# A two-stage fused kernel on one core: cross-partition sums and maxima moved off GpSimd, and a new table of durations in its list scheduler

## The chip, the core and the metric

The kernel runs on one core of a Trainium2 chip. The metric is the device time of one execution in microseconds (us), lower is better. Engines are named as the profile names them: PE is TensorE (matmul), DVE is VectorE, ACT is ScalarE, POOL is GpSimd, SP is SyncE, which here issues every DMA. Each engine works through its own instructions in order and waits on semaphores for the others.

## What is computed

Two residual steps over `x` of 2 batches x 1024 tokens x 2048 features:

```python
def fake_quant(x, scale, zp):
    q = jnp.clip(jnp.round(x / s + z), 0.0, 255.0)
    return (q - z) * s

# step 1: quantized product with the context
x = x + matmul(fake_quant(layernorm(x), x1_scale, x1_zp),      # (2, 1024, 2048)
               fake_quant(ctx_4096, x2_scale, x2_zp))          # (2, 2048, 2048)

# step 2: a dense layer with 8 low-rank experts, the best 2 per token
xf = layernorm(x)
probs = softmax(xf @ W_router.T)
topk_p, topk_i = top_k(probs, 2); topk_p = topk_p / sum(topk_p)
h = einsum('td,erd->ter', xf, lora_A)
lora_out = einsum('ter,eor,te->to', h, lora_B, w) * 2.0        # w: topk_p at topk_i
x = x + (xf @ W_base.T + b_base) + lora_out
```

`W_base` is 2048 x 2048, `lora_A` 8 x 16 x 2048, `lora_B` 8 x 2048 x 16, all f32.

## The kernel before

**Tiling.** A tile is 128 tokens; there are 8 per batch (`NT`), taken in 4 pairs (`NP`, index `p`). The output columns are cut in four of 512 (`C`), or two halves of 1024 (`HD`, index `cp`).

**First gemm.** For each token tile `load_x` and `ln1` load `x`, take the statistics on DVE (`bn_stats`), refine the reciprocal square root with three Newton steps (on DVE for the very first tile, on POOL for the others, L576 to L586), quantize to `q` (uint8, ACT only), subtract the zero point to `qn` (f16, ACT or DVE), and transpose with a DMA to `at`. For each column block `load_b` loads a pair of context rows `bs`, quantizes to `u` (uint8, L626, DVE only) and subtracts the zero point to `b` (f16, ACT or DVE, L627). `gemm1` multiplies (`g`, L636) and adds into `x` on DVE (L657), `square` on ACT gathers the sum of squares for the second layer norm.

**Between.** `ln2` makes the scale and shift of the second layer norm per pair (statistics on DVE, Newton on POOL except for the last pair). `y_prep` makes, per pair, six operand tiles for a Strassen-like second gemm: normalized quarters `yt`, sums and differences of them (`comb`, L749), and from each a high and a low f16 part in `nat` (L740 and L742), transposed by a DMA to `y` (L744). `x` goes to DRAM as `spill` where its buffers are needed. That makes 24 large transposes per batch.

**Second gemm.** For each half `cp` of the columns come four groups `grp` of products (`GROUPS`), each over 8 steps `k`. `w_step` loads rows of `W_base` (`wt`, `wb`, `ws`), combines them on DVE (L918, L928, L932, L939, L942) and splits them into a high and a low f16 part scaled by `gW` (`hi`, ACT or DVE; `lo`, DVE, L902). `g2` multiplies (L1032), adds the low-rank part (L1046), and evicts on DVE (L1057) into `xr` or `x`. `hmm` makes the router and low-rank products (L790, L794), `router` picks the experts.

**The scales.** `gW` is a power of two from the largest sum of squares of `W_base` rows and from the largest `lora_B`. `prep_bmax` takes the largest absolute value per partition on DVE (L484, L488), then the maximum over the 128 partitions with a custom POOL instruction (L491, `partition_all_reduce`), and `fin` makes `lB` from it (L497 to L502). `w_norm(cp)` squares every row of one half of `W_base` (`wn`, `wj`, L525 and L527), sums along the row on DVE (L534), sums over partitions with the same custom POOL instruction (L537), and makes `gW`, `uW`, `sB` (L542 to L549). Every `hi` and `lo` of that half, and every eviction L1057, needs them. It runs once before the second gemm of batch 0 and once, for the other half, in group 3 of its first half.

**The order.** Nothing is issued in program order. `Plan.add` collects tasks with engine, duration and buffers, and `Plan.order` is a list scheduler in the program: `rank` gives each task a latest start from the due times of PE's tasks, and the loop keeps a clock, a busy time per engine, and a count of free buffers per tag (48 of tag `u`, 8 PSUM banks). At every event each free engine takes the most urgent ready task whose buffers are free. A task with two possible engines (`affine` without `only`) goes to ACT if ACT is idle at that instant, else to DVE. The instructions are then issued in order of planned start, so a planned start fixes each engine's queue; semaphores keep the real execution right where it runs later than planned. For a DMA the plan keeps `dma_free`, the time at which the DMA engines have moved all that was issued; SP issues no further one while that is more than 2.5 us (`DEPTH`) ahead or 8 (`LANES`) are in flight.

The old times for a DMA, at L242 and in the two helpers:

```python
dma_free = max(now + 1.1, dma_free) + t.dma
t.done = dma_free + 2.0
# load:      SP 0.47, dma = bytes / 360e3
# transpose: SP 1.25, dma = 0.896 * cols / 1024
```

Of the kernel before, what the change touches and what calls it, by code (L numbers as in the profile page):

```python
# [11 lines left out]
F32 = mybir.dt.float32  # L12
# [54 lines left out]
DMA_SLACK = 3.0  # L67

# [14 lines left out]
class Task:  # L83
    __slots__ = ("eng", "dur", "durs", "fn", "preds", "succs", "prio", "cap", "bufs", "left",
                 "ready", "start", "done", "dma", "seq", "pe", "far", "need")


class Plan:
# [3 lines left out]
    def add(self, eng, dur, fn, r=(), w=(), prio=None, cap=None, dma=None, far=None):  # L92
# [7 lines left out]
        t.far = far  # L100
# [40 lines left out]
    def order(self):  # L141
# [6 lines left out]
        dma_free = 0.0  # L148
        lag = 0.0
# [43 lines left out]
        while todo:  # L193
# [8 lines left out]
            for eng in busy:  # L202
                while busy[eng] <= now:
# [35 lines left out]
                    end = now + t.dur  # L239
                    busy[eng] = end  # L240
                    wake(end)
                    if t.dma is not None:  # L242
                        dma_free = max(now + 1.1, dma_free) + t.dma
                        t.done = dma_free + 2.0
                        lanes = [x for x in lanes if x > now] + [t.done]
                    else:
                        t.done = end + 0.2
# [22 lines left out]
def xattn_ffn_kernel(ctx, tc, x, cx, scal, wT, bias, arT, bT, out):  # L270
# [41 lines left out]
    nc.gpsimd.memset(magic, 0x5F3759DF)  # L312
    iota = const.tile([P, E], F32)
# [17 lines left out]
    def load(dst, dst_ap, src, nbytes, w, r=(), **kw):  # L331
        add("SP", 0.47, lambda: nc.sync.dma_start(dst_ap(), src() if callable(src) else src),
            r=r, w=w, dma=nbytes * P / 360e3, **kw)

    def transpose(dst, src, r, w, cols, **kw):
        add("SP", 1.25, lambda: nc.sync.dma_start_transpose(dst(), src()),
            r=r, w=w, dma=0.896 * cols / 1024, **kw)

    def affine(dst, src, n, r, w, scale=None, bias=None, only=None, **kw):
# [19 lines left out]
        durs = {"ACT": n * 0.00083 + 0.19 + 0.09 * ptrs, "DVE": n * 0.00053 + 0.08 + 0.06 * ptrs}  # L359
# [49 lines left out]
    def prep_lora(when):  # L409
        a32 = []  # L410
        ps = bank("arn")
        on = buf("u", [P, P], F32, "ones")
        add("POOL", 0.2, lambda: nc.gpsimd.memset(on.ap(), 1.0), w=[on])
        for q in range(4):
# [11 lines left out]
            def mm(q=q, s=v):  # L426
                for k in range(4):
                    nc.tensor.matmul(
                        ps.ap()[:, :AR], on.ap(), s.ap()[:, k, :], start=q + k == 0,
                        stop=q + k == 6,  # L430
                    )

            add("PE", 1.0, mm, r=[v, on], w=[ps], prio=when + q)
# [35 lines left out]
        for q in range(2):  # L469
# [3 lines left out]
            add("DVE", 0.6,  # L473
# [4 lines left out]
    def prep_bmax():  # L478
        m = buf("sm", [P, 52], F32, "sm_bmax")
        for h in range(2):  # L480
            s = buf("u", [P, HD], F32, f"bms_{h}")
            load(s, s.ap, bT[:, h * HD : (h + 1) * HD], HD * 4, [s])
            add("DVE", 1.13,
# [6 lines left out]
        add("POOL", 1.5,  # L490
            lambda: nc.gpsimd.partition_all_reduce(  # L491
                b_max, m.ap()[:, 2:3], P, bass_isa.ReduceOp.max), r=[m], w=[bmax_b])

        def fin():
            a = m.ap()
            i = a[:, 3:4].bitcast(I32)
# [7 lines left out]
        add("DVE", 0.8, fin, r=[lora_b], w=[m, bmax_b])  # L504
# [8 lines left out]
    def w_norm(cp, when):  # L513
        acc = buf("wacc", [P, 24], F32, f"wacc_{cp}", KT)
        for n, k in enumerate(range(KT - 1, -1, -1)):
# [6 lines left out]
            def sq(eng, s=s, d=d, k=k):  # L522
# [8 lines left out]
            add({"ACT": 1.2, "DVE": 1.3}, 0, sq, r=[s], w=[d, (acc, [k])],  # L531
# [4 lines left out]
        add("POOL", 1.5,  # L536
            lambda: nc.gpsimd.partition_all_reduce(  # L537
                acc.ap()[:, 21:22], acc.ap()[:, 20:21], P, bass_isa.ReduceOp.add), w=[acc])

        def fin():  # L540
            a = acc.ap()
            pow2(a[:, 22:23], a[:, 21:22], a)  # L542
# [8 lines left out]
        add("DVE", 1.5, fin, r=[bmax_b, lora_b], w=[acc, (scale_b, [cp])])  # L551
# [14 lines left out]
    def ln1(S, b, i):  # L566
# [3 lines left out]
        for h in range(2):  # L570
            add("DVE", 1.2, lambda h=h: stats(xt[h], s, 0, h), r=[xt[h]], w=[s])
# [43 lines left out]
    def load_b(S, b, c):  # L615
        for j in range(4):
            bp = buf("u", [P, 4, C], F16, f"b_{b}_{c}_{j}", 2)
            S["b", c, j] = bp
            for h in range(2):
# [6 lines left out]
                affine(u.ap, s.ap, HD, [s], [u], scale=r2, bias=z2, only="DVE")  # L626
# [3 lines left out]
    def gemm1(S, b, i, c, t):  # L630
# [30 lines left out]
        add("DVE", 0.78, evac, r=[ps], w=[(xb, [c % 2]), (s, [j])], cap=t + KT * MM + EV1)  # L661
# [21 lines left out]
        add("ACT", 1.3, lambda: square(c // 2), r=[xb], w=[(s, [j]), sq])  # L683
# [41 lines left out]
    def y_prep(S, b, p):  # L725
# [10 lines left out]
        def emit(o, t):  # L736
# [4 lines left out]
            add("DVE", 1.13,  # L741
# [6 lines left out]
        def comb(dst, a, c, op):  # L748
            add("DVE", 1.13, lambda: nc.vector.tensor_tensor(dst.ap(), a.ap(), c.ap(), op),  # L749
# [438 lines left out]
```

## Time and profile before

| | us |
|---|---|
| median of three runs | 966.87 |
| lowest, highest run | 965.12, 968.43 |
| span of the profiled execution | 965.8 |

What the page adds, of the lines not shown further on:

| part of the page | what it says |
|---|---|
| granted PE clock in tenths, by the 40 slices | 7 in the second slice (24 to 48 us), 9 in all others |
| chain that ended last, share by engine | PE 62%, DVE 19%, POOL 6%, DMA 5%, issue 5%, ACT 2%, SP queue 1% |
| DMA queue | 225,456 packets, 242.33 MB, 83.0% of 16 engines' span |
| u, L357 on DVE | 64 instructions, 808 ns each |
| b, L346 on ACT | 47 instructions, 1143 ns each |
| q, L346 on ACT | 32 instructions, 1232 ns each |
| nat by L742, 1024 wide, on DVE | 56 instructions, about 1217 ns each |
| landing of a 512 KB load, from issue | 6.4 (wt) to 9.9 (bs) us |
| landing of a transpose, from issue | 4.3 to 5.9 us |

A row of a timeline gives start, duration, engine, line, operation, what it writes and reads, and, in brackets, the idle time of the engine before it with what ended that. SPq is SP's queue: its duration is the time for which the DMA instructions held the queue. Several like instructions in a row are merged (x5). In a table of windows each engine's busy time stands beside the count of its instructions.

### The profile page before, as it was taken

Reading aid. Unit: us, or ns where it says so; the run is one execution under the profiler, and the core shown is the slowest. Engines: PE = TensorE matmul, PEld = TensorE weight load, DVE = VectorE, ACT = ScalarE, POOL = GpSimd, SP = SyncE. Lnnn points to the kernel's source line nnn. Section 1 sums busy time; section 2 is a strip of 40 time slices with the busy share of each in tenths; the row PEclk is TensorE's granted clock in tenths of the full one; section 3 lists DMA queues with packets and bytes.
Section 4 is the critical chain, followed back from the end, with each engine's and each line's share of the span. In section 5 each row is a group of like instructions: output and inputs, shape, how many; then the busy total and the mean of one; then the engine's idle time right before and its main releaser. Section 6 shows DMA issues by size and latency. Waiting matters only on the chain.

```text
span 965.8 us, 12426 instructions
## 1 busy us (share of the span) xinstructions
PE 913.9 (95%) x4478; PEld 431.5 (45%) x4478; DVE 734.1 (76%) x1229; ACT 379.9 (39%) x440; POOL 100.0 (10%) x353
## 2 busy tenths in 40 slices
PE   3699998997999999999999999997898999999998
PEld 1245445454444444444444444545543444444443
DVE  7579887996988876999555778987597876699231
ACT  3466785641425422243555644641230321225000
POOL 3405431000000000005220223000000000000000
PEclk9799999999999999999999999999999999999999
DMA  9999999899899986966999979899978479695011
GB/s 319 246 392 336 303 313 243 214 189 233 246 302 389 360 312 244 363 219 242 239 273 356 319 190 228 245 215 185 255 180 262 163 272 325 207 356 171 34 66 66
DMA packets 225518, 243.12 MB, mean 252 GB/s; under 512 B 160944, under 2 KB 162992, under 8 KB 225456
## 3 DMA queue, kind: packets, MB, share of 16 engines
q1 hardware_dynamic: 225456, 242.33, 83.0%
q8 instruction: 35, 0.57, 0.2%
q14 instruction: 27, 0.22, 0.1%
HBM read 172.03 MB, written 31.46 MB: 211 GB/s over the span
## 4 chain that ended last, share of the span: by engine, by line
PE 62%; DVE 19%; POOL 6%; DMA 5%; issue 5%; ACT 2%; SPq 1%; DVEq 0%; POOLq 0%; ACTq 0%
PE X L1032 28%; PE Y L1032 19%; PE g L636 11%; DVE yt_a L749 2%; DVE nat_s L742 2%; DVE w L902 2%; PE X L1046 2%; PE Y L1046 2%; DVE nat_a L742 2%; DMA wb<-in_wT_dram 2%; DVE xr L1057 1%; POOL sm L399 1%; POOL sm L395 1%; DMA wt<-in_wT_dram 1%; DVE x L657 1%
## 5 line engine op out<-in xcount | busy, mean ns | idle before, releaser
L636 PE MATMUL g<-b,at 128*128 128x512 f16 x1024 | 228.5, 386 | 9.2 <-ACT b L346 7.4
L1032 PEld LDWEIGHTS <-y_s 128*128 128x128 f16 x1536 | 149.8, 98 | 192.4 <-issue 9.9
L1032 PE MATMUL Y<-w,y_s 128*128 128x512 f16 x768 | 207.1, 380 | 5.7 <-DVE hf L809 2.8
L1032 PE MATMUL X<-w,y_s 128*128 128x512 f16 x768 | 207.7, 381 | 4.3 <-DVE w L902 2.6
L1032 PE MATMUL X<-w,y_a 128*128 128x512 f16 x768 | 190.4, 380 | 4.5 <-DVE w L902 2.6
L1032 PEld LDWEIGHTS <-y_a 128*128 128x128 f16 x1152 | 112.5, 98 | 144.9 <-issue 7.3
L636 PEld LDWEIGHTS <-at 128*128 128x128 f16 x1024 | 101.4, 99 | 133.6 <-issue 17.5
L346 ACT ACTIVATE w<-wb,gW 128x1024 f16<-128x1024 f32 x59 | 67.4, 1147 | 190.3 <-DVE wb L932 94.3
L1032 PE MATMUL Y<-w,y_a 128*128 128x512 f16 x384 | 103.3, 379 | 3.8 <-DVE xr L1057 2.7
L902 DVE SCALAR_TENSOR_TENSOR w<-wb,gW,w 128x1024 f16<-128x1024 f32 x64 | 81.6, 1278 | 11.7 <-ACT w L346 11.3
L357 DVE TENSOR_SCALAR u<-bs,rec,sc 128x1024 uint8<-128x1024 f32 x64 | 50.9, 808 | 27.5 <-DMA bs<-in_cx_dram 22.0
L346 ACT ACTIVATE b<-u,nz 128x1024 f16<-128x1024 uint8 x47 | 53.0, 1143 | 44.7 <-DVE u L357 40.2
L1057 DVE SCALAR_TENSOR_TENSOR xr<-X,uW,xr 128x512 f32<-128x512 f32 x70 | 50.5, 744 | 25.7 <-PE X L1046 23.2
L1057 DVE SCALAR_TENSOR_TENSOR xr<-Y,uW,xr 128x512 f32<-128x512 f32 x45 | 33.2, 742 | 36.0 <-PE Y L1046 36.0
L657 DVE SCALAR_TENSOR_TENSOR x<-g,s,x 128x512 f32<-128x512 f32 x64 | 47.4, 745 | 10.3 <-PE g L636 10.1
L346 ACT ACTIVATE q<-x,sm 128x1024 uint8<-128x1024 f32 x32 | 38.0, 1232 | 34.0 <-POOL sm L584 29.2
L928 DVE TENSOR_TENSOR wb<-wt 128x512 f32<-128x512 f32 x32 | 21.9, 687 | 34.4 <-DMA wt<-in_wT_dram 28.7
L939 DVE TENSOR_TENSOR wb<-wb,wt 128x1024 f32<-128x1024 f32 x32 | 38.7, 1218 | 11.5 <-DMA wb<-in_wT_dram 11.5
L742 DVE TENSOR_TENSOR nat_s<-yt_a,nat_s 128x1024 f16<-128x1024 f32 x32 | 38.3, 1217 | 5.5 <-ACT nat_s L346 5.5
L367 DVE BATCH_NORM_STATS2 sm<-x 128x6 f32<-128x512 f32 x64 | 40.4, 680 | 2.5 <-DMA x<-in_x_dram 2.4
L346 ACT ACTIVATE nat_s<-yt_a 128x1024 f16<-128x1024 f32 x27 | 27.8, 1049 | 33.3 <-DMA y_s<-nat_s 14.9
L790 PE MATMUL ph<-ar,y_a 128*128 128x272 f16 x192 | 37.0, 284 | 3.9 <-DVE xr L1057 2.1
(157 smaller groups left out, 901.8 us busy)
## 6 DMA issues: line engine op xcount, KB each, us to landing
wt<-in_wT_dram SPq DMA_DIRECT2D x88, 512.0 KB, 6.4
bs<-in_cx_dram SPq DMA_DIRECT2D x64, 512.0 KB, 9.9
wn<-in_wT_dram SPq DMA_DIRECT2D x32, 512.0 KB, 7.6
wb<-in_wT_dram SPq DMA_DIRECT2D x32, 512.0 KB, 8.1
x<-in_x_dram SPq DMA_DIRECT2D x30, 512.0 KB, 8.3
spill<-x SPq DMA_DIRECT2D x28, 512.0 KB, 4.0
xr<-spill SPq DMA_DIRECT2D x28, 512.0 KB, 6.8
out_dram<-xr SPq DMA_DIRECT2D x24, 512.0 KB, 4.2
```

The lines of the kernel that those rows point to most:

```text
L346: nc.scalar.activation(o, i, AF.Copy if c is None else AF.Identity, scale=1.0 if a is None else a, bias=0.0 if c is None else c,)
L357: nc.vector.tensor_scalar(o, i, a, c, ALU.mult, ALU.add)
L367: nc.vector.bn_stats(st[:, 2 * h + c], b.ap()[:, c * C : (c + 1) * C])
L636: nc.tensor.matmul(ps.ap(), aT.ap()[:, k, :], S["b", c, k // 4].ap()[:, k % 4, :], start=k == 0, stop=k == KT - 1,)
L657: nc.vector.scalar_tensor_tensor(xs, ps.ap(), s12, xs, ALU.mult, ALU.add, accum_out=s.ap()[:, o : o + 1])
L742: lambda: nc.vector.tensor_tensor(n.ap()[:, 1], t.ap(), n.ap()[:, 0], ALU.subtract), r=[t], w=[n])
L790: nc.tensor.matmul(ph.ap()[:, : 2 * AR], y[half].ap()[:, 0, k, :], ar[:, kr, :], start=kk == 0, stop=False,)
L902: lambda: nc.vector.scalar_tensor_tensor(w.ap()[:, 1, lo:up], src(), g, w.ap()[:, 0, lo:up], ALU.mult, ALU.subtract),
L939: lambda: nc.vector.tensor_tensor(bot.ap(), bot.ap(), top.ap(), ALU.subtract),
L1032: nc.tensor.matmul(ps.ap(), y.ap()[:, a, k, :], w.ap()[:, q, j * C : (j + 1) * C], start=k == 0 and fresh and i == 0, stop=k == HK - 1 and ...
L1046: nc.tensor.matmul(ps.ap(), hT.ap()[:, 2 * p + tt, a], lb.ap()[:, q], start=False, stop=i == 2, skip_group_check=True,)
L1057: nc.vector.scalar_tensor_tensor(xs, ps.ap(), uW[:, cp : cp + 1], xs, ALU.mult, ALU.add)
```

## The change

Four things change together.

1. `w_norm`: the sum over partitions is a matmul of a constant 128x128 tile of ones (f32) with the column of partial sums, into a PSUM bank; `fin` reads the bank. The constant is set once at the start; `prep_lora` uses it instead of a tile of its own.
2. `prep_bmax`: the column of maxima is stored to DRAM, loaded back as one row broadcast to all partitions, and reduced by DVE along the row.
3. `load_b`: `u` may go to ACT or DVE.
4. The scheduler's times: a rate of 405e3 bytes per us for loads, landing times, a rule for transposes (flag `turn`: it holds SP until everything issued before has landed), and new durations for most tasks.

```diff
+RATE = 405e3
+LAND = 1.9
+TURN_LAND = 2.5
+NEXT = {"DVE": 0.08, "ACT": 0.1}
...
                     end = now + t.dur
+                    if t.dma is not None:
+                        if t.turn:
+                            end = max(end, land)
+                            dma_free = max(dma_free, end + t.dma)
+                            t.done = end + TURN_LAND
+                        else:
+                            dma_free = max(end + 0.2, dma_free) + t.dma
+                            t.done = dma_free + LAND
+                        land = max(land, t.done)
+                        lanes = [x for x in lanes if x > now] + [t.done]
+                    else:
+                        t.done = end + 0.1
+                        end -= NEXT.get(eng, 0.0)
                     busy[eng] = end
                     wake(end)
-                    if t.dma is not None:
-                        dma_free = max(now + 1.1, dma_free) + t.dma
-                        t.done = dma_free + 2.0
-                        lanes = [x for x in lanes if x > now] + [t.done]
-                    else:
-                        t.done = end + 0.2
...
+    ones = const.tile([P, P], F32)
+    nc.gpsimd.memset(ones, 1.0)
...
     def load(dst, dst_ap, src, nbytes, w, r=(), **kw):
-        add("SP", 0.47, lambda: nc.sync.dma_start(dst_ap(), src() if callable(src) else src),
-            r=r, w=w, dma=nbytes * P / 360e3, **kw)
+        add("SP", 0.42, lambda: nc.sync.dma_start(dst_ap(), src() if callable(src) else src),
+            r=r, w=w, dma=nbytes * P / RATE, **kw)
 
     def transpose(dst, src, r, w, cols, **kw):
-        add("SP", 1.25, lambda: nc.sync.dma_start_transpose(dst(), src()),
-            r=r, w=w, dma=0.896 * cols / 1024, **kw)
+        add("SP", 1.35 + 0.25 * cols / 1024, lambda: nc.sync.dma_start_transpose(dst(), src()),
+            r=r, w=w, dma=0.5 * cols / 1024, turn=True, **kw)
...
-        durs = {"ACT": n * 0.00083 + 0.19 + 0.09 * ptrs, "DVE": n * 0.00053 + 0.08 + 0.06 * ptrs}
+        durs = {"ACT": n * 0.00083 + 0.19 + 0.09 * ptrs, "DVE": n * 0.00053 + 0.145 + 0.06 * ptrs}
...
-        add("POOL", 1.5,
-            lambda: nc.gpsimd.partition_all_reduce(
-                b_max, m.ap()[:, 2:3], P, bass_isa.ReduceOp.max), r=[m], w=[bmax_b])
+        d = Buf("dram", lambda: dram.tile([P, 1], F32, name="bmax"))
+        row = buf("u", [P, P], F32, "bmax_row")
+        load(d, d.ap, lambda: m.ap()[:, 2:3], 4, [d], r=[m])
+        load(row, row.ap, lambda: d.ap().rearrange("p o -> o p").to_broadcast([P, P]), P * 4,
+             [row], r=[d])
 
         def fin():
             a = m.ap()
+            nc.vector.tensor_reduce(b_max, row.ap(), AX.X, ALU.max)
...
-        add("POOL", 1.5,
-            lambda: nc.gpsimd.partition_all_reduce(
-                acc.ap()[:, 21:22], acc.ap()[:, 20:21], P, bass_isa.ReduceOp.add), w=[acc])
+        ps = bank(f"wsum_{cp}")
+        add("PE", 0.2,
+            lambda: nc.tensor.matmul(
+                ps.ap()[:, :1], ones, acc.ap()[:, 20:21], start=True, stop=True),
+            r=[acc], w=[ps], prio=when + WN_STEP * KT)
...
-                affine(u.ap, s.ap, HD, [s], [u], scale=r2, bias=z2, only="DVE")
+                affine(u.ap, s.ap, HD, [s], [u], scale=r2, bias=z2)
...
-        add("DVE", 0.78, evac, r=[ps], w=[(xb, [c % 2]), (s, [j])], cap=t + KT * MM + EV1)
+        add("DVE", 0.75, evac, r=[ps], w=[(xb, [c % 2]), (s, [j])], cap=t + KT * MM + EV1)
...
-            add("DVE", 1.13,
+            add("DVE", 1.22,
                 lambda: nc.vector.tensor_tensor(
                     n.ap()[:, 1], t.ap(), n.ap()[:, 0], ALU.subtract), r=[t], w=[n])
```

The other durations move in the same manner: 1024-wide `tensor_tensor` and reduces on DVE 1.13 to 1.22, 512-wide 0.6 to 0.69, the low part of the weights from 0.14 to 0.215 plus the same slope, the eviction of the second gemm 0.72 to 0.75, `square` on ACT 1.3 to 1.33, the high part of `lb` on ACT 0.62 to 0.72 and its low part on DVE 0.67 to 0.75, the two squares of `w_norm` 1.2 and 1.3 to 1.25 and 1.31. Due times, horizons and buffer counts stay as they are.

## The prediction

> **What bounds the kernel now.** I read the head of the page, then busy time by stage (window sums), then PE's waits in each stage, then the timelines of POOL, DVE, PE and the DMA queue where PE stands still.
>
> ```profile
> span 965.8 us, 12426 instructions
> PE 913.9 (95%) x4478; PEld 431.5 (45%) x4478; DVE 734.1 (76%) x1229; ACT 379.9 (39%) x440; POOL 100.0 (10%) x353
> ```
>
> PE is busy 913.9 of 965.8, so whatever a better order can win lies in the other 51.9. The window sums (stretch, length, busy PE, PEld, DVE, ACT, POOL with counts, granted clock, DMA share, GB/s) say where they are:
>
> ```profile
> 0.00:41.30 41.30, 17.55 (x55) 6.61 (x56) 27.99 (x66) 17.21 (x16) 17.83 (x61) 0.90 0.95 292
> 41.30:160.00 118.70, 118.70 (x599) 58.56 (x599) 96.17 (x223) 83.73 (x111) 35.23 (x114) 0.98 1.04 316
> 160.00:245.00 85.00, 74.47 (x435) 38.92 (x433) 75.23 (x118) 34.08 (x40) 0.40 (x1) 0.98 0.95 226
> 245.00:620.00 375.00, 373.90 (x1771) 171.75 (x1769) 300.32 (x498) 164.78 (x188) 46.55 (x177) 1.00 0.89 280
> 620.00:745.00 125.00, 112.29 (x621) 57.51 (x620) 97.29 (x164) 35.74 (x40) 0.00 (x0) 0.99 0.91 231
> 745.00:966.00 221.00, 216.97 (x1006) 98.11 (x1003) 137.04 (x165) 44.38 (x47) 0.00 (x0) 1.00 0.52 184
> ```
>
> Length less PE busy: 23.7 idle at the start, 0 in the first gemm, 10.5 in 160:245 (batch 0 passing into the second gemm), 1.1, 12.7 in 620:745 (batch 1 doing the same), 4.0 in the tail. Inside the first gemm and the two long stretches PE already runs without a break, so DVE or ACT time saved there is worth nothing by itself.
>
> In 160:245 DVE is busy 75.2 of 85, and PE waits for what it makes. Just before, POOL holds DVE up (timelines; start, duration, engine, line, operation, in brackets the idle time before and what ended it):
>
> ```profile
> 143.06 1.24 POOL L491 PARTITION_ALL_REDUCE b_max<-sm_bmax  x1 [10.54 <-DVE sm_bmax L488]
> 151.85 0.25 POOL L389 TENSOR_SCALAR sm<-sm 128x2 f32<-128x2 f32 x1 [7.56 <-issue]
> ...
> 146.56 0.16 DVE L708 TENSOR_TENSOR sm<-magic,sm 128x2 int32<-128x2 int32 x1
> 156.31 1.54 DVE L357 TENSOR_SCALAR yt_a<-x,sm 128x1024 f32<-128x1024 f32 x2 [5.32 <-POOL sm L721]
> 162.78 0.15 DVE L404 TENSOR_SCALAR wacc<-wacc 128x1 int32<-128x1 int32 x1 [1.18 <-POOL wacc L537]
> ...
> 167.79 0.59 PE L1032 MATMUL X<-w,y_a 128*128 128x512 f16 x2 [2.62 <-DVE w L902]
> ```
>
> The Newton step at 151.85 had its input at 146.72 (L708), but POOL did nothing that the profile shows for 7.56 after the custom reduce: the reduce costs far more than its 1.24. DVE then waits 5.32 for Newton and 1.18 for the second reduce, and PE waits for the weight tile made late.
>
> The other loss is the one DMA queue. Three times a row of transposes keeps the weight rows behind it, and DVE idles for a row (7.72 and 7.39 in two of them):
>
> ```profile
> 217.44 14.10 SPq L336 DMA_TRANSPOSE y_s<-nat_s  x5
> 231.60 0.83 SPq L332 DMA_DIRECT2D wt<-in_wT_dram  x1
> 237.20 0.69 DVE L928 TENSOR_TENSOR wb<-wt 128x512 f32<-128x512 f32 x1 [7.72 <-DMA wt<-in_wT_dram]
> 666.78 13.68 SPq L336 DMA_TRANSPOSE y_s<-nat_s  x5
> 686.25 0.69 DVE L928 TENSOR_TENSOR wb<-wt 128x512 f32<-128x512 f32 x1 [7.39 <-DMA wt<-in_wT_dram]
> 713.95 11.46 SPq L336 DMA_TRANSPOSE y_s<-nat_s  x4
> ```
>
> Those 14 transposes hold the queue for 39.24, 2.80 each. The old planner books 1.25 for one on SP, so it puts rows behind them too late.
>
> **The change, part by part.**
>
> *Custom reduces out of POOL.* Removed: DVE's 5.32 and 1.18, 6.5. PE's waits in 155:245 are 5.2 on L902 and 0.8 on ACT's w, 6.0, and 4.5 on transposes landing. Those 6.0 are what the late DVE makes, so I take **-6.0**; ends 0 (the transposes would end the same waits) and -6.5. The later reduce at 328.7 lies in a stretch without PE idle: 0.
>
> The Trainium skill's GPSIMD Engine Reference, Instruction dispatch, says that the first call of a freshly loaded kernel pays about 6 us of code loading that no instruction shows. Here the silent time is 7.56; by the page the wait would be about 1.6 shorter, and the gain about -4.4 (an estimate). The same page's Engine selection speaks against the change: a reduction along partitions belongs on GPSIMD. The row of 7.56 weighs more for a reduce that is called three times.
>
> *Maximum by DRAM bounce.* Added: a store of 128 values and a broadcast load, both on SP, and a reduce over 128x128 on DVE (the 128x128 reduce L438 takes 0.285). Each transfer lands after between 1.7 (the 2 KB of scal) and 9.9 (bms), two in series 3.4 to 19.8, so with L488 done at 142.9 the row is there between 146.3 and 162.7. DVE read b_max at 150.26: a wait of 0 to 12.4 if `fin` keeps its place, but its result is first needed by L545 at 163.35, and the planner may move it. With 4 to 5 for each transfer (spill 4.0, transposes 4.9) it is there at about 152, so **+1.5**, with the reduce +0.3. The load also waits on SP for the store, and the transposes behind it wait as long; their cover is that DVE and ACT have nat tiles to make. 0 to +3, taken as 0.
>
> The skill's DMA: Bandwidth & Descriptors, Anatomy of one DMA, gives about 2 us fixed per transfer (measured there on the GpSimd path). Two in series would be 4, the row would be there at 147 and cost only its 0.3.
>
> *Sum by ones product.* Two fp32 matmuls with N = 1. The nearest rows are L428's 128x136 f32 matmul, 0.279, recorded twice per instruction: at most 0.6 each. At 158.6 PE is doing router products and the sum is earlier than POOL's. At 328 PE is the bound and in order: queued there is the second gemm itself, all of whose DVE evictions wait behind it, and if `wacc` (L534, 328.3) is late against plan, PE stands until it is there. The row loads behind it land 7.6 after issue, the old plan allows 4.6 (1.1 + 1.46 + 2.0). 0 to +3 for each product; taken **+0.3**, since the planner may place it late.
>
> *u on either engine.* 64 instructions of 0.81 on DVE may become about 1.23 on ACT (the same form, L346 q, takes 1.23). From 41 to 160 PE is covered either way: 0. At the start POOL's Newton for tiles 2 and 3 takes 8.25 each (19.28 to 27.52 to 35.7) against 4.4 for the first, its operations 0.5 to 1.3 instead of 0.19 while DVE runs TENSOR_SCALAR, and ACT's q, qn, b wait for it before PE can run at 41.27. Fewer u on DVE free POOL; but a u on ACT can also stand behind a q that waits 4.7. PE's gaps there are 1.75 + 3.99 + 3.43. Ends -4 and +5; taken **-1**.
>
> *Durations.* DVE's numbers hardly move: 1.22 less NEXT's 0.08 is 1.14 for 1.13. Evictions get 0.67 for 0.78, ACT 0.1 less per instruction. Large is SP: a 2048-column transpose 1.85 for 1.25, and it holds SP until all earlier loads have landed. The planner then knows the 2.8 that it now underrates, and should spread the rows between. PE loses 0.36 + 1.65 at 240, 2.79 + 0.52 at 688 and 1.89 at 733 behind the three runs, 7.2; the rest of 620:745 is short waits on DVE's evictions (hf, xr). I take half of the 7.2 and a little of the rest: **-1** in 160:245 and **-4** in 620:745. Ends -12 (most of 4.5 + 12.7 goes) and +17 (below). This is the largest unknown: every queue is ordered anew.
>
> Sum: 965.8 - 6.0 + 1.8 + 0.3 - 1 - 1 - 4 = 955.9. The profiled span stands 1.1 under the median 966.87 (the runs spread 3.3), so **957**.
>
> **The rivals.**
>
> *A: same time.* The POOL wait goes, and transposes or the bounce end the same PE waits; the order gains nothing. For it: 4.5 of 160:245 waits on transposes already, DMA share 0.95. Against: DVE, not DMA, feeds the 2.62 and its neighbours. 965.8 - 6 + 4.5 + 0.3 = 964.6, with 1.1 **966**.
>
> *B: slower, longer runs of transposes.* Since a planned transpose now waits for every earlier landing, the planner may stack transposes and send weight rows after them, in 200:245 or 640:740. A run of 5 leaves about 6 of its 14 covered by rows in hand (14.1 - 7.7); a run of 8 lasts 8.4 longer, all of it on DVE and soon on PE. From 965.8 - 6 + 2.1 = 961.9, one such run gives 970, two 979: with 1.1 **971 to 980, say 975**. It decides from an excess of 3.9, 1.4 transposes more in a run. For it: such runs exist; none of the due times (EV1, SP_T, LAG3, WFAR) is refitted. Against: the old plan makes these runs because it books too little.
>
> *C: it does not do what it says.* u stays on DVE, since ACT must be idle at that instant, and the start is as before: forecast + 1, inside its range.
>
> **How the numbers follow.** Forecast (C within): 0.60, own range 944 to 963. A: 0.12. B: 0.28. No change means within 0.3%, 964.0 to 969.8, about what a measurement of this kernel can tell apart. Faster is the forecast and 0.01 of A's lower edge, 0.61; same the rest of A, 0.11; slower is B, 0.28. The low end puts the good ends together: 955.9 + 5 - 12 (order) - 3 (start at -4) - 1.5 (no wait for the bounce) - 0.5 (POOL at -6.5) = 943.9, with 1.1 945, and one more for the unknown order: 944. The high end takes in B's first run and half of the way to the second: 975. About 0.06 is left out below and 0.13 above.
>
> **What would show it.** No POOL custom reduce and no silent 7 on POOL at 144 to 152; DVE without the 5.32; gW ready some 3 to 5 before 163.6, and PE's idle in 160:245 at 4 to 6 instead of 10.5. `fin` shows a DVE wait of 1 to 2 on the row. PE idle in 620:745 at 8 to 9. Runs of transposes shorter than 14. Some u on ACT, and PE's unbroken run from about 40. Wrong if PE idle in 160:245 and 620:745 together stays above 23.2, if a run of transposes exceeds 17, or if PE stands before a 1-column product.

## The result: the other way, and the profile after

The changed kernel takes 973.76 us (median of five runs, 971.54 to 976.71) against 966.87. The ratio is 1.0067, with a 95% interval of 1.0046 to 1.0088: slower by more than the 0.3% that a measurement can tell apart. The forecast was 957. The time lies inside the stated range, which ends at 975, but on the side that had a chance of 0.28, and not by the mechanism that was put there.

The head of the page and the shares by engine of the chain that ended last, in the kernel after:

```profile
span 971.9 us, 12447 instructions
...
PE 913.8 (94%) x4482; PEld 432.1 (44%) x4482; DVE 720.3 (74%) x1211; ACT 407.0 (42%) x459; POOL 93.4 (10%) x350
...
PE 56%; DVE 18%; DMA 14%; issue 5%; POOL 3%; ACT 3%; SPq 2%; DVEq 0%; ACTq 0%; POOLq 0%
```

PE is busy as long as before (913.8 and 913.9), so the 6.1 us by which the span grew are PE standing still: 58.1 against 51.9. In the chain DMA has gone from 5% to 14% and POOL from 6% to 3%. The window sums of the kernel after (stretch, length, busy PE, PEld, DVE, ACT, POOL with counts, granted clock, DMA share, GB/s) say in which stage:

```profile
0.00:41.30 41.30, 18.51 (x70) 7.41 (x70) 28.03 (x67) 20.71 (x18) 15.24 (x62) 1.00 0.85 265
41.30:160.00 118.70, 112.49 (x552) 54.12 (x552) 89.94 (x205) 86.94 (x110) 29.29 (x104) 0.98 1.03 307
160.00:245.00 85.00, 73.26 (x440) 40.90 (x441) 70.68 (x116) 36.73 (x45) 2.52 (x9) 0.93 1.04 230
245.00:620.00 375.00, 369.87 (x1710) 166.98 (x1708) 289.57 (x485) 170.76 (x187) 46.33 (x176) 1.00 0.87 278
620.00:745.00 125.00, 119.29 (x697) 63.40 (x695) 101.65 (x172) 48.75 (x55) 0.00 (x0) 0.99 0.97 247
745.00:972.00 227.00, 220.41 (x1018) 99.25 (x1016) 140.45 (x169) 43.11 (x46) 0.00 (x0) 1.00 0.52 181
```

Length less PE busy, and beside it the same before:

| stretch | PE idle after | before |
|---|---|---|
| 0 to 41.3 | 22.8 | 23.7 |
| 41.3 to 160 | 6.2 | 0 |
| 160 to 245 | 11.7 | 10.5 |
| 245 to 620 | 5.1 | 1.1 |
| 620 to 745 | 5.7 | 12.7 |
| tail | 6.6 | 4.0 |

The hoped-for gain in 620:745 came, and is larger than predicted (7.0 for 4). It is paid away elsewhere, and above all in one hole that straddles 160 us: 4.1 of it in the second row, 3.9 in the third. Without that hole the table would sum to 50.0, less than before.

The hole can be followed backwards through the timelines of the kernel after, each a view of one engine (start, duration, engine, line, operation, in brackets the idle time before and what ended it). PE stands 8.07 us until a transposed operand tile lands:

```profile
163.94 0.41 PE L807 MATMUL ph<-ar,y_a 128*128 128x272 f16 x1 [8.07 <-DMA y_a<-nat_a]
```

The hole costs more than its 8.07. In the 10.2 us from 158.8 on the granted clock, third from the end of the row, was 0.50, and this product takes 0.41 where the same took 0.28 at 149.78:

```profile
158.80:169.00 10.20, 5.06 (x30) 3.93 (x31) 8.01 (x18) 7.34 (x12) 3.47 (x12) 0.50 1.06 241
```

The tile that PE waited for was not made late. In the plan it is the fourth `nat_a` tile on DVE and the fourth to be transposed on SP. DVE had it ready at 142.9, but its transpose was issued only at 158.89, because the transpose ahead of it held SP's queue for 9.95 (DVE's and SP's timelines, each transpose by itself):

```profile
141.67 1.22 DVE L759 TENSOR_TENSOR nat_a<-yt_a,nat_a 128x1024 f16<-128x1024 f32 x1
...
148.84 9.95 SPq L350 DMA_TRANSPOSE y_a<-nat_a  x1
...
158.89 1.83 SPq L350 DMA_TRANSPOSE y_a<-nat_a  x1
```

The queue came free at 158.8, just as the last of the row loads issued ahead of it landed (issued at 147.58, landed 11.4 later, at 159.0). DVE and ACT stood still over the same loads, though not on the way to this wait. DVE made its next tile after standing 6.77 for ACT:

```profile
149.66 1.22 DVE L759 TENSOR_TENSOR nat_a<-yt_a,nat_a 128x1024 f16<-128x1024 f32 x1 [6.77 <-ACT nat_a L360]
...
164.69 0.28 DVE L510 TENSOR_REDUCE b_max<-bmax_row 128x1 f32<-128x128 f32 x1 [0.58 <-DMA bmax_row<-bmax]
```

ACT's piece of that tile (L360, at 148.59) was queued behind a square-and-sum of a `W_base` row, which waited 8.02 for the row:

```profile
147.54 1.06 ACT L540 ACTIVATE wn<-wn 128x1024 f32<-128x1024 f32 x1 [8.02 <-DMA wn<-in_wT_dram]
```

And the rows were issued directly behind the store of the maxima:

```profile
132.89 0.55 SPq L346 DMA_DIRECT2D bmax<-sm_bmax  x1
133.49 14.41 SPq L346 DMA_DIRECT2D wn<-in_wT_dram  x9
148.84 11.89 SPq L350 DMA_TRANSPOSE y_a<-nat_a  x2
160.82 1.05 SPq L346 DMA_DIRECT2D bmax_row<-bmax  x1
```

The nine row loads hold SP's queue for 14.41, and two transposes come only at 148.84. The store itself, 512 bytes, is the odd one. The tile view of `bmax` gives for the store and the row load:

```profile
DMA to landing us min/median/max: 3.9/7.0/10.2
```

The 3.9 is the row load, the 10.2 the store: as long as a load of 512 KB takes in the slowest group before (`bs`, 9.9 in the middle and 11.8 at most). The window from 134 to 143, when it was in flight, shows what passed through the DMA engines meanwhile:

```profile
134.00:143.00 9.00, 9.00 (x43) 4.09 (x42) 5.95 (x10) 2.37 (x2) 2.27 (x11) 1.00 0.79 38
```

The last two numbers are the ones to read: the engines count as busy for 0.79 of the time, and move 38 GB/s. In every stage of the table above they move 181 to 307. In the packet records a packet of 4,096 bytes takes 0.8 to 2.9 us on average in each 2 us from 134 to 144, and 0.16 to 0.17 from 146 to 160.

The first suspicion was therefore not the latency of the bounce, which `fin` felt with 0.58 only, but that **the store of 128 four-byte values stops every transfer behind it**. The rivals to it: that the new order as a whole, made by the new durations, is the loss and the hole is one place where it shows; and that the reduces taken off POOL never gave anything.

### The profile page after: what moved, and what is told of

The parts are those of the page before. It is cut to its first block, busy times and chain, and to the rows that moved or that the text cites. A ratio compares the mean times of both kernels' runs of the same rounds, so it can differ in the third digit from the quotient of the medians.

```text
span 971.9 us, 12447 instructions
## 1 busy us (share of the span) xinstructions
PE 913.8 (94%) x4482; PEld 432.1 (44%) x4482; DVE 720.3 (74%) x1211; ACT 407.0 (42%) x459; POOL 93.4 (10%) x350
## 4 chain that ended last, share of the span: by engine, by line
PE 56%; DVE 18%; DMA 14%; issue 5%; POOL 3%; ACT 3%; SPq 2%; DVEq 0%; ACTq 0%; POOLq 0%
PE X L1049 23%; PE Y L1049 14%; PE g L653 14%; DMA wb<-in_wT_dram 4%; DVE w L919 4%; DMA bs<-in_cx_dram 3%; DMA wn<-in_wT_dram 2%; DVE wb L956 2%; PE X L1063 2%; DMA wt<-in_wT_dram 2%; DVE xr L1074 1%; DVE wb L959 1%; PE ph L807 1%; DVE xr L995 1%; PE Y L1063 1%
## 5 line engine op out<-in xcount | busy, mean ns | idle before, releaser
L653 PE MATMUL g<-b,at 128*128 128x512 f16 x1024 | 225.2, 381 | 8.4 <-DMA at<-qn 6.1
L360 ACT ACTIVATE w<-wb,gW 128x1024 f16<-128x1024 f32 x62 | 70.7, 1147 | 183.7 <-DVE wb L959 82.0
L360 ACT ACTIVATE u<-bs,sc,rec 128x1024 uint8<-128x1024 f32 x45 | 55.6, 1238 | 25.8 <-DMA bs<-in_cx_dram 23.1
L403 POOL TENSOR_SCALAR sm<-sm 128x1 f32<-128x1 f32 (+1 forms) x21 | 5.1, 241 | 490.6 <-DVE sm L393 418.6
L369 DVE TENSOR_SCALAR b<-u,nz 128x1024 f16<-128x1024 uint8 x40 | 29.9, 751 | 26.2 <-ACT u L360 26.1
L360 ACT ACTIVATE q<-x,sm 128x1024 uint8<-128x1024 f32 x32 | 38.3, 1232 | 20.0 <-POOL sm L601 12.6
L692 ACT ACTIVATE sq<-x,sm 128x1024 uint8<-128x1024 f32 x32 | 36.4, 1139 | 12.2 <-DVE x L674 6.1
L360 ACT ACTIVATE nat_s<-yt_a 128x1024 f16<-128x1024 f32 x29 | 29.6, 1048 | 27.1 <-DMA y_a<-nat_a 14.3
```

Of the source, the lines that this page charges most:

```text
L360: nc.scalar.activation(o, i, AF.Copy if c is None else AF.Identity, scale=1.0 if a is None else a, bias=0.0 if c is None else c,)
L369: nc.vector.tensor_scalar(o, i, c, None, ALU.add)
L653: nc.tensor.matmul(ps.ap(), aT.ap()[:, k, :], S["b", c, k // 4].ap()[:, k % 4, :], start=k == 0, stop=k == KT - 1,)
L692: nc.scalar.activation(sq.ap(), xb.ap(), AF.Square, bias=a[:, 22 + j : 23 + j], accum_out=a[:, 24 + 2 * j + h : 25 + 2 * j + h],)
```

## The experiments

Each kernel was timed against the kernel before on one chip; ratios are to that, with 95% intervals. The chips differ (medians of the kernel before between 965.77 and 967.55), so ratios are compared, not microseconds.

**Leave out the store.** The kernel after, with the same planned order: the store's place in the plan is kept but issues nothing, and the row is loaded from 128 values of `lora_B`. The maximum over partitions is therefore not computed; `lB` gets another value.

```diff
-        load(d, d.ap, lambda: m.ap()[:, 2:3], 4, [d], r=[m])
-        load(row, row.ap, lambda: d.ap().rearrange("p o -> o p").to_broadcast([P, P]), P * 4,
-             [row], r=[d])
+        add("SP", 0.42, lambda: None, r=[m], w=[d], dma=4 * P / RATE)
+        load(row, row.ap, bT[0:1, 0:P].to_broadcast([P, P]), P * 4, [row], r=[d])
```

> The changed kernel with every queue in its planned order, but the store of the 128 maxima is left out: the row is loaded from 128 values of lora_B instead, so the scale lB comes from other data. Theory 1 (the store of 128 four-byte values to DRAM keeps the weight loads behind it from moving for about 9 us, 134 to 143; ACT waits 8.0, DVE 6.8, PE 8.1 in turn): the loads issued after 133.5 land in 4 to 6 us instead of 11, their 4 KB packets take 0.2 us instead of 2.2 to 2.9, PE's gap of 8.07 at 156 shrinks to 0 to 2, the span falls from 971.9 to 962 to 967. Theory 2 (the new order, with nine weight loads ahead of two transposes, makes that gap): the gap stays above 6 and the span within 2 of 971.9.

Measured: 963.14, ratio 0.9974 [0.9956, 0.9992]. From 1.0067 that is 0.93% of 966, about 9 us, for one transfer of 512 bytes. The same window:

```profile
134.00:143.00 9.00, 9.00 (x44) 4.08 (x42) 6.05 (x10) 5.50 (x7) 2.63 (x11) 1.00 1.01 332
```

332 GB/s for 38, and ACT does 5.50 us of work there for 2.37. The first of the two transposes is issued at 139.45 for 148.84, and PE's gap of 8.07 is one of 2.05 here. The store, and not the order, makes the hole: the order is the same.

**Only the two reduces.** The kernel before with the ones product and the bounce, old durations, `u` on DVE.

```diff
+        load(d, d.ap, lambda: m.ap()[:, 2:3], 4, [d], r=[m])
+        load(row, row.ap, lambda: d.ap().rearrange("p o -> o p").to_broadcast([P, P]), P * 4,
+             [row], r=[d])
...
+            lambda: nc.tensor.matmul(
+                ps.ap()[:, :1], ones, acc.ap()[:, 20:21], start=True, stop=True),
```

> The kernel before with the ones product and the DRAM bounce alone (old durations, u on DVE only). Theory 1: the silent 7.56 on POOL is gone, but a hole of some 9 us in DMA traffic opens behind the four-byte store, wherever it now stands; what POOL gives back is taken again, 964 to 972 against 965.8, and PE's idle in 160:245 is 8 or more. Theory 2: only the POOL wait goes, 958 to 962, no hole in the traffic.

Measured: 975.99, ratio 1.0099 [1.0070, 1.0127]. The loss is there without the new durations. Here the planner put things differently, and DVE meets both ends of it:

```profile
154.45 1.22 DVE L530 SCALAR_TENSOR_TENSOR wj<-wn 128x1024 uint8<-128x1024 f32 x1 [6.03 <-DMA wn<-in_wT_dram]
...
163.11 0.29 DVE L498 TENSOR_REDUCE b_max<-bmax_row 128x1 f32<-128x128 f32 x1 [7.42 <-DMA bmax_row<-bmax]
```

The store landed after 8.9, and from 139 to 148 the DMA engines moved 32 GB/s; then the two transposes that the planner had set ahead of the row load held SP until 160.00. So `fin` waits 7.42, for which the prediction had 1.5 (ends 0 and 12.4). Of the 8.7 us by which this span exceeds the one before, only 3.1 are PE idle. The other 5.6 are PE busy for longer, at a mean granted clock of 0.982 for 0.989.

**`u` on either engine, alone.** The kernel before without `only="DVE"`.

```diff
-                affine(u.ap, s.ap, HD, [s], [u], scale=r2, bias=z2, only="DVE")
+                affine(u.ap, s.ap, HD, [s], [u], scale=r2, bias=z2)
```

> The kernel before with u on either engine alone. Both theories: PE is covered from 41 to 160, so only the start and a reshuffled order show: 962 to 970 against 965.8, some 40 of the 64 u on ACT. If it stands above 970, the u on ACT is the cause and both theories fall.

Measured: 964.10, ratio 0.9989 [0.9973, 1.0004]: about -1.1, and no change is inside the interval.

**All durations, alone.** The kernel before with every new time; the custom reduces stay and `u` stays on DVE.

```diff
+RATE = 405e3
+LAND = 1.9
+TURN_LAND = 2.5
+NEXT = {"DVE": 0.08, "ACT": 0.1}
...
-        add("SP", 1.25, lambda: nc.sync.dma_start_transpose(dst(), src()),
-            r=r, w=w, dma=0.896 * cols / 1024, **kw)
+        add("SP", 1.35 + 0.25 * cols / 1024, lambda: nc.sync.dma_start_transpose(dst(), src()),
+            r=r, w=w, dma=0.5 * cols / 1024, turn=True, **kw)
```

> The kernel before with the new durations and the transpose rule alone (custom POOL reduces kept, u on DVE only). Theory 1: the new order is no worse than the old: it wins some 7 in 620:745 and gives back some 5 in short gaps of the long stretches, 958 to 968. Theory 2: the new order is the loss: 970 or more, with an idle stretch of PE of over 6 near 156.

Measured: 967.66, ratio 1.0027 [1.0008, 1.0045]. PE idle in 620:745 falls from 12.7 to 7.9, as predicted (8 to 9), yet the whole is no faster. Two runs further down take it apart.

**Spread the store.** Like the first experiment, but the store is made: the same 128 values of four bytes, each into a 512-byte line of its own in DRAM. The row again comes from `lora_B`, so the maximum is left out here too.

```diff
-        d = Buf("dram", lambda: dram.tile([P, 1], F32, name="bmax"))
+        d = Buf("dram", lambda: dram.tile([P, P], F32, name="bmax"))
-        load(d, d.ap, lambda: m.ap()[:, 2:3], 4, [d], r=[m])
+        load(d, lambda: d.ap()[:, 0:1], lambda: m.ap()[:, 2:3], 4, [d], r=[m])
```

> As e1_no_store (changed kernel, order kept, row from 128 values of lora_B), but the store is made: 128 values of four bytes, each into its own 512-byte line of a DRAM tile instead of 512 bytes side by side. If the writes are slow because they fall into the same few lines one after another, the hole in the traffic goes: the loads behind land in 4 to 6 us, the span is 961 to 966. If any four-byte write to DRAM is slow, the hole of some 9 us and PE's gap of 8 stay, the span is 970 to 974.

Measured: 966.49, ratio 0.9986 [0.9971, 1.0001]. The tile view of `bmax`, then the window, then SP's timeline:

```profile
DMA to landing us min/median/max: 2.2/2.2/2.2
```

```profile
134.00:143.00 9.00, 9.00 (x44) 4.05 (x43) 6.05 (x10) 5.23 (x7) 2.90 (x11) 1.00 0.95 299
```

```profile
133.21 0.59 SPq L346 DMA_DIRECT2D bmax<-sm_bmax  x1
133.85 5.51 SPq L346 DMA_DIRECT2D wn<-in_wT_dram  x9
140.29 10.78 SPq L350 DMA_TRANSPOSE y_a<-nat_a  x2
```

The same number of writes of the same size lands in 2.2 for 10.2, and the nine loads hold SP for 5.51 for 14.41. The loads held SP for the same 5.51 where no store was made. So neither the count nor the size of the writes makes the hole; what differs is that all 128 go into the same 512 contiguous bytes. One pitch was tried, and the larger tile may also lie elsewhere in DRAM, so a place that is slow by itself is not ruled out. Why the memory or the DMA engines answer so, no record shows. Against leaving the store out the intervals overlap: the spread store may cost nothing.

**POOL free, order unchanged.** The kernel before, with each custom reduce replaced by an ordinary one-column instruction at the same booked duration. It copies the maximum of its own partition and multiplies its own sum by 128, so nothing is reduced over partitions.

```diff
-            lambda: nc.gpsimd.partition_all_reduce(
-                b_max, m.ap()[:, 2:3], P, bass_isa.ReduceOp.max), r=[m], w=[bmax_b])
+            lambda: nc.gpsimd.tensor_scalar(
+                b_max, m.ap()[:, 2:3], 1.0, None, ALU.mult), r=[m], w=[bmax_b])
```

> The kernel before with every queue in its planned order, but the three custom reduces are replaced by an ordinary one-column POOL instruction (the maximum and the sum over partitions are left out, the sum replaced by 128 times the partition's own). This is the term that the prediction priced at -6.0. If that holds: no silent 7.56, DVE without its 5.32 and 1.18, the span 959 to 961 against 965.8. If transposes end the same PE waits (rival A): 963 to 966.

Measured: 968.05, ratio 1.0000 [0.9987, 1.0012]. This is the predicted -6.0, and it is 0. The silent 7.56 on POOL is gone (POOL's timeline: Newton starts when its input is there), and DVE's wait for Newton falls from 5.32 to 2.02 (DVE's timeline):

```profile
145.34 0.21 POOL L389 TENSOR_SCALAR sm<-sm 128x2 f32<-128x2 f32 x1 [2.26 <-DVE sm L706]
```

```profile
151.95 1.53 DVE L357 TENSOR_SCALAR yt_a<-x,sm 128x1024 f32<-128x1024 f32 x2 [2.02 <-POOL sm L721]
...
195.41 1.22 DVE L742 TENSOR_TENSOR nat_a<-yt_a,nat_a 128x1024 f16<-128x1024 f32 x1 [4.20 <-ACT nat_a L346]
```

What DVE wins at 152 it waits at 195, in a place where it did not wait before. PE's waits between 155 and 245 in this kernel (what waited for what, us in total, times, longest) say who sets the pace instead:

```profile
PE Y L1032 <- DMA y_s<-nat_s: 2.8, 3, 1.8
PE X L1032 <- DVE w L902: 2.2, 2, 1.6
PE X L1032 <- DMA y_a<-nat_a: 2.0, 1, 2.0
PE X L1032 <- DMA y_s<-nat_s: 1.4, 1, 1.4
PE ph L790 <- DMA y_s<-nat_s: 1.1, 1, 1.1
PE X L1032 <- ACT w L346: 0.3, 1, 0.3
```

Waits on weights 6.0 before, now 2.5; waits on transposes 4.5 before, now 7.3. The row of five transposes on SP stands where it stood (218.59 for 14.09, before 217.44 for 14.10). The same end is reached through the transposes.

**A maximum without DRAM.** The kernel after, with identity times the column of maxima on DVE, a ones product of that on PE, and `fin`'s reduce reading the PSUM bank. The maximum is computed again, and no transfer is needed.

```diff
+        add("DVE", 0.3,
+            lambda: nc.vector.tensor_scalar(dg.ap(), eye, m.ap()[:, 2:3], None, ALU.mult),
+            r=[m], w=[dg])
+        add("PE", 0.4,
+            lambda: nc.tensor.matmul(ps.ap()[:, :P], ones, dg.ap(), start=True, stop=True),
+            r=[dg], w=[ps])
...
-            nc.vector.tensor_reduce(b_max, row.ap(), AX.X, ALU.max)
+            nc.vector.tensor_reduce(b_max, ps.ap()[:, :P], AX.X, ALU.max)
```

> The changed kernel with the bounce replaced by a second product: DVE scales an identity by the column of maxima, PE multiplies it by the ones, and every partition holds all 128 maxima in PSUM, which DVE reduces. New order. If the store is all that the change lost: 959 to 965, with PE's idle in 160:245 at 8 or less. If it stays above 970, the store is not the only loss.

Measured: 962.97, ratio 0.9942 [0.9919, 0.9965]: faster than before, and 1.25% below the change as made.

**The same with the old durations** (ones product, identity product, `u` on either engine, in the kernel before).

```diff
+        ps = bank("bmaxp")
+        add("DVE", 0.3,
...
-                affine(u.ap, s.ap, HD, [s], [u], scale=r2, bias=z2, only="DVE")
+                affine(u.ap, s.ap, HD, [s], [u], scale=r2, bias=z2)
```

> The kernel before, with its old durations, with the ones product, the identity product of e7_diag_product and u on either engine. Since the new durations alone gave 0.27% back and u alone won 0.1%, this should be the fastest: 956 to 963. If it is not faster than e7_diag_product, the old durations are no better once the store is gone.

Measured: 965.50, ratio 0.9975 [0.9963, 0.9988], not the fastest, as was expected of it. So with a maximum that doesn't touch DRAM, the whole change is a gain with either set of durations; between the two sets the intervals meet (0.9963 and 0.9965), which isn't enough to call the new ones better.

**The head of the first tile as one task.** In the kernel after PE's first matmul (a warm-up product) comes at 16.40 us, before at 14.56: DVE takes statistics of the second tile before it seeds the first tile's Newton steps. This comes with the new DMA times: of the two halves tried further down, they alone have it at 17.24, the engine durations alone at 14.99. To the identity version was added that the second half of the first tile's statistics, its seed and its Newton steps are one DVE task.

```diff
-        add("DVE" if fast else "POOL", 2.2 if fast else 4.0, newton, w=[s])
+        def head():
+            stats(xt[1], s, 0, 1)
+            rstd_seed(s, 1)
+            newton()
+        if fast:
+            add("DVE", 4.3, head, r=[xt[1]], w=[s])
```

> As e7_diag_product, and the first tile's second statistics, its seed and its Newton steps are one task, so that no other tile's statistics stand between them on DVE. In the changed kernel PE's first matmul is at 16.40 instead of 14.56 because DVE takes the second tile's statistics in between, which the new load rate lets land too early. If that start counts: PE begins at 13 to 14 and the time falls by 1.5 to 3 from e7_diag_product, to about 960. If the start is set by POOL's Newton for the later tiles, the time stays within 1 of e7_diag_product.

Measured: first matmul at 13.38, but 960.25 and ratio 0.9950 [0.9934, 0.9967], no different from 0.9942. A start 3.36 earlier than in the identity version (16.74) brought nothing that shows: after the warm-up PE's next two gaps are 3.84 and 5.13, the second for transposed tiles of `q`, where the identity version has 4.08 and 1.85.

**The durations in two halves.** First only the DMA times and the transpose rule, then only the new durations of DVE, ACT and PE tasks with `NEXT`, each alone in the kernel before.

```diff
+                        if t.turn:
+                            end = max(end, land)
+                            dma_free = max(dma_free, end + t.dma)
+                            t.done = end + TURN_LAND
+                        else:
+                            dma_free = max(end + 0.2, dma_free) + t.dma
+                            t.done = dma_free + LAND
```

> The kernel before with the new times for loads and transposes alone (rate, landing, the turn rule); engine durations, reduces and u as before. The prediction gave this part -5. If the rule is what e4_times_only showed in 620:745: PE's idle there falls to about 8, one gap of some 5 at 640 stands for several short ones, the time is 960 to 968. If the rule alone makes it slower than e4_times_only, the engine durations hid a loss.

```diff
+                        t.done = end + 0.1
+                        end -= NEXT.get(eng, 0.0)
...
-            add("DVE", 1.13,
+            add("DVE", 1.22,
...
-        add("ACT", 1.3, lambda: square(c // 2), r=[xb], w=[(s, [j]), sq])
+        add("ACT", 1.33, lambda: square(c // 2), r=[xb], w=[(s, [j]), sq])
```

> The kernel before with the new engine durations alone (DVE and ACT tasks, the 0.08 and 0.1 of NEXT); loads and transposes as before. The prediction gave this part next to nothing: 964 to 970, the stages of the kernel before with 12 to 13 of PE idle in 620:745. If it stands above 970, the engine durations are the loss inside e4_times_only.

Measured: the DMA rule 962.71, ratio 0.9966 [0.9952, 0.9981]; the engine durations 969.67, ratio 1.0046 [1.0028, 1.0064]. They go opposite ways. PE idle in 620:745 is 6.2 with the rule, 11.8 with the durations, 12.7 before. One wait tells them apart, that of PE for a transposed tile near 640 us. PE's waits from 630 to 652, with the engine durations:

```profile
PE X L1038 <- DMA y_a<-nat_a: 4.7, 1, 4.7
```

and with the DMA rule:

```profile
PE X L1042 <- DMA y_a<-nat_a: 0.9, 1, 0.9
```

It is 3.6 to 5.3 in all seven kernels that have the new engine durations (5.1 in the kernel after) and 0.9 to 2.7 in all seven, the kernel before (1.4) among them, that have the old ones. But that wait alone doesn't account for the loss: the stage round it idles no longer with the engine durations than before (11.8 and 12.7). What they add in the profile lies in 41.3:160 (2.6 for 0) and 245:620 (3.4 for 1.1).

**DMA rule with old engine durations**, ones and identity product, `u` on either engine, the head as one task.

```diff
+                        if t.turn:
+                            end = max(end, land)
...
+            add("DVE", 4.2, head, r=[xt[1]], w=[s])
```

> Everything that won, without what lost: the kernel before with the new times for loads and transposes, its old engine durations, the ones product, the identity product of e7_diag_product, u on either engine, and the first tile's head as one task as in e9_diag_start. If the parts add up (e10_dma_rule won 0.3%, e11_engine_times lost 0.5%), it is faster than e9_diag_start: 953 to 959. If the parts don't add, because each new plan draws its small gaps anew, it is between 958 and 964.

Measured: 961.09, ratio 0.9936 [0.9912, 0.9959]. The wait near 640 is 1.5. The rule's -0.34% and the -0.25% of the identity version with old durations would make the ratio 0.9941; that lies inside the interval, so these two gains add up as far as can be measured. The head as one task gave nothing to see here either. This one, the identity version and the one with the single head task are all 0.5 to 0.6% faster than the kernel before, and their intervals overlap, so no one of them is shown to be the best.

## Why the prediction was wrong, step by step

**The DRAM bounce: the step that failed.** It was priced as two latencies, taken as +1.5 with +0.3 for the reduce, and the queue behind it was "0 to +3, taken as 0". About +9 us (0.93%) came from the store alone. The latency was indeed small in the kernel after (0.58), and the term is not a latency at all: a store of 512 bytes slowed every other transfer for some 9 us, so that work with no tie to the maximum came late. The failure lies in the queue term. The prediction saw that "the transposes behind it wait as long" and covered them with "DVE and ACT have nat tiles to make". That covers nothing: the tile that PE waited for had been made 16 us before its transpose was issued, and PE waits for the transpose. ACT couldn't go on with the next tiles either, since its next instruction needed a loaded row. The prediction bounded a landing by medians of ordinary transfers, 1.7 to 9.9, and 10.2 lies close to that. What it never asked is what a slow store does to the loads issued after it.

The Trainium skill's DMA: Bandwidth & Descriptors, Anatomy of one DMA, was cited for some 2 us per small transfer. The page measured that for DMAs issued from GpSimd; these were issued from SP. The spread store, 2.2, agrees with it. The contiguous one, 10.2, does not, nor do the row loads, 3.9 and 3.1, and the measurement decides.

**Custom reduces off POOL: -6.0 predicted, 0 measured** (-0.13% to +0.12%). The reading of the silent 7.56 was right: with an ordinary instruction in the reduce's place it is gone. The sum failed in "those 6.0 are what the late DVE makes". PE's waits on weights fell by 3.5, and its waits on transposes rose by 2.8. This is rival A's mechanism, given 0.12, and the lower end, 0, of the stated bounds. The evidence was on the page: 4.5 of that stage's waits on transposes already, and a DMA share of 0.95. The argument against it, that DVE feeds the 2.62, looked at who ends each wait and not at who is next.

**Durations: -5 predicted, +0.27% measured (about +2.6).** The half that was argued from the transposes had the right sign and was over-rated: -0.34% alone, about -3.3 us for -5. In 620:745 PE's idle fell by 6.5, where 4 was forecast, but in 160:245 it rose from 10.5 to 12.7, where -1 was forecast, and 41.3:160 got 3.0. The other half was dismissed with "DVE's numbers hardly move", and costs +0.46%. Where it costs that is not shown: the long wait near 640 marks every kernel with these durations, yet its stage is no slower for it. Which of the durations matters was not tried. Each number moved little, but a list scheduler decides by comparing times, so a small shift can change which task is taken.

**Ones product: +0.3 predicted.** PE never waits for it. It runs at 169.2 and at 339.0 in the kernel after, in PE's timeline:

```profile
339.03 0.28 PE L553 MATMUL wsum<-wacc,ones 128*128 128x1 f32 x2
```

**`u` on either engine: -1 predicted, -1.1 measured**, not distinguishable from nothing. Of the 64 instructions 45 went to ACT, and of the 47 `b` that were there 23 went to DVE.

**The signs that were named.** Silent POOL time gone: yes. DVE without its 5.32 for Newton: gone, but 6.77 for ACT took its place. `gW` 3 to 5 us earlier: it came at 173.38, 10 later than before. PE idle in 160:245 at 4 to 6: 11.7, and 4.1 of the hole lie ahead of 160. PE idle in 620:745 at 8 to 9: 5.7. Runs of transposes shorter than 14: hardly, 13.04, 13.56 and 10.57 for 14.10, 13.68 and 11.46. None of the three conditions for "wrong" was met, though the forecast was wrong: PE idle of both stages together 17.4, no run over 17, no wait ahead of a one-column product. They watched the planner, and the loss was in a transfer. Rival B gave the right time by luck: none of the three runs of transposes that it was built on grew.

**What the parts leave open.** The single edits sum to 0.99 - 0.11 + 0.27 = +1.15%, the whole is +0.67%. Each edit makes a new order, so the effects need not add, and differences of up to half a per cent between orders are not explained here one by one. Nor is it shown what the memory does with 128 writes to the same lines.

## What to carry to other kernels

A tiny transfer is priced by what it does to the transfers around it as well as by its own latency: keep four-byte stores of many partitions out of one small stretch of DRAM (a pitch of 512 bytes cost nothing that shows here), or don't go through DRAM at all, where an identity product and a ones product on PE do the same. Before crediting a removed wait, take it away with the order kept (a cheap instruction in its place) and look which wait is next; here that showed 0 for 6. And test each half of a table of durations alone: one half gained a third of a per cent, the other lost nearly half.

## What was not expected of the hardware

A store of 128 values of four bytes to 512 contiguous bytes of DRAM landed after 10.2 us (8.9 in a second kernel), and during that time the core's DMA engines moved 38 GB/s instead of some 300; with each value in its own 512 bytes it landed after 2.2, and the loads behind it held SP no longer than without a store (5.51). The engines' busy share in that window, 0.79, looks healthy: only the bytes moved give it away. And PE's pause of 8.07 us cost more than itself: from 158.8 to 169.0 the granted clock was 0.50.
